# An earlier beginning, and the last four row blocks as rows, in a two-layer graph kernel

## The chip, the cores and the metric

The kernel runs on one core of one Trainium2 chip. The metric is the device time of one execution in microseconds. Four runs of the kernel before gave 2417.09 to 2418.88 us, with a median of 2418.69.

A core has five engines with a queue each: TensorE (matmuls, in profiles PE, its weight loads PEld), VectorE (DVE), ScalarE (ACT), GpSimd (POOL) and SyncE (SP), which here only issues transfers. Transfers are issued from the queues of SP, ScalarE and GpSimd.

## The reference, cut to what matters

There are 16 graphs of 1024 nodes with 128 features. Each goes through two layers, and each layer ends in a residual and a norm.

```python
# layer 0
h = x @ Ww.T + Wb
e = (h @ A) @ h.T;  e = e + e.T
att = softmax(where(adj > 0, e, 0), axis=1) * adj
hp = relu(att @ h)
i, f, o = (sigmoid(hp @ w_u + x @ w_x) for each of three gates)
x1 = layernorm(x + o * tanh(i * hp + f * x))          # eps 1e-5
# layer 1, four heads
h = x1 @ conv_w[hd] + conv_b[hd]
s = tanh(adj * (h @ attn_w[hd] @ h.T))
m = relu(mean over heads of relu(s @ h))
out = layernorm(x1 + relu(m + x1))                    # eps 1e-5
```

## The kernel before

A graph's 1024 nodes are eight blocks of 128. The kernel writes out the order of all instructions by hand; each engine works through its own in that order. Graph b's layer 1 is a loop over 32 steps (four heads of eight blocks, `layer1_step`), and between its steps stand pieces of layer 0 of the following graphs, named by letters in lists such as `"E1 S4 A0 T3"`: `L` load a block of adj, `E` find its edges (adj > 0), `Q` project to q, `H`/`h` multiply and add for h, `S` a row block of scores, `T` turn the part above the diagonal to below it, `A` mask with the edges, take the maximum and the exponential, `B` multiply with adj, divide and start the product with h. Graph 0 has no earlier graph to hide behind. Its layer 0 stands by itself at the start, and its order is in the two `run(first, ...)` lines.

**The beginning.** From A and Ww the kernel makes a_sym = A + A.T, s_ww = a_sym Ww and q_w = Ww.T s_ww, so that q = x q_w + c is one product. `keep_at_work(n)` gives TensorE n matmuls on zeros, whose result nobody reads. `finish_weights` adds the last column of wb_row and the gates' columns gate_x. A and Ww and Wb are loaded from ScalarE's queue, the three gate rows rows_x from GpSimd's, and xT, the eight blocks of adj, x and everything later from SP's. Graph 0's edges are found by VectorE, apart from blocks 5 and 6, which GpSimd finds. The turned copies of score block 0 wait in PSUM and are placed by VectorE (`place_first_score`, L397); those of the other blocks are copied by ScalarE (L376).

`small(...)` hands out four PSUM banks in turn, so a fifth request waits until the first has been read.

**The end.** Layer 1 sums the heads' results turned, features on partitions, in `sum_t`. For the last head of the last graph, tanh's results stay in `kept`. The first 512 nodes are multiplied within the steps. The other 512 follow in three parts, quarter (256 nodes), eighth and rest (128 each), by `last_back`: the head's h is stationary and `kept` moves, so the result has features on partitions; VectorE adds it to the sum (L667), and `last_end` turns it back on TensorE (L698), makes the residual on VectorE (L699, L702), and runs the norm. The norm takes statistics on VectorE (L221, L223, L225), the power -1/2 on GpSimd (L226), and applies both: on ScalarE for half and quarter (L232, L235), on VectorE for eighth and rest (L237). Its numbers are in the pools `mv` and `rs`, two buffers each, used in turn by all norms.

Of the kernel before, what the change touches and what calls it, by code (L numbers as in the profile page):

```python
# [11 lines left out]
F32 = mybir.dt.float32  # L12
# [3 lines left out]
ALU = mybir.AluOpType  # L16
# [8 lines left out]
def two_layer_adjacency_kernel(  # L25
# [48 lines left out]
    a_in = sb.tile([P, P], F32, tag="hz", name="a_in", bufs=4)  # L74
    nc.scalar.dma_start(a_in, A)
    ww_in = sb.tile([P, P], F32, tag="hz", name="ww_in", bufs=4)
    nc.scalar.dma_start(ww_in, Ww)
    wb_col = consts.tile([P, 1], F32, name="wb_col")

    wb_in = sb.tile([1, P], F32, tag="x1T", name="wb_in")  # L80
    nc.scalar.dma_start(wb_in, Wb.rearrange("(o d) -> o d", o=1))
    rows_x = sb.tile([3, P], F32, tag="s1", name="rows_x", bufs=4)
    for g, w in enumerate((wi_x, wf_x, wo_x)):
        nc.gpsimd.dma_start(rows_x[g : g + 1], w.rearrange("(o d) -> o d", o=1))
    rows_u = sb.tile([3, P], F32, tag="turn", name="rows_u", bufs=2)


# [53 lines left out]
        for _ in range(n):  # L141
            nc.tensor.matmul(idle[:, :P], warm[:, :P], warm[:, :P], start=True, stop=True)  # L142

    keep_at_work(7)
    pa, pb = small("p_a"), small("p_s")
    nc.tensor.transpose(pa[:, :P], a_in, ident)
    nc.vector.tensor_add(a_sym, pa[:, :P], a_in)
    keep_at_work(2)
    nc.tensor.matmul(pb[:, :P], a_sym, ww_in, start=True, stop=True)
    nc.vector.tensor_copy(s_ww, pb[:, :P])  # L150
    pc, pw = small("p_b"), small("p_ww")
    nc.tensor.transpose(pw[:, :P], ww_in, ident)
    nc.tensor.matmul(pc[:, P : P + 1], wb_in, ones[:, 0:1], start=True, stop=True)
    nc.tensor.matmul(pc[:, :P], ones, wb_in, start=True, stop=True)
    nc.vector.tensor_copy(wb_col, pc[:, P : P + 1])
    nc.scalar.copy(wwT, pw[:, :P])
    nc.scalar.copy(wb_row[:, :D], pc[:, :P])
    nc.gpsimd.tensor_copy(b_wide, wb_col.to_broadcast([P, P]))
    pq, pc = small("p_q"), small("p_c")
    nc.tensor.matmul(pq[:, :P], s_ww, ww_in, start=True, stop=True)  # L160
    nc.vector.tensor_copy(q_w, pq[:, :P])
    nc.tensor.matmul(pc[:, 0:1], s_ww, wb_col, start=True, stop=True)
    nc.tensor.matmul(pc[:, 1:2], a_sym, wb_col, start=True, stop=True)
    nc.vector.tensor_copy(c_col, pc[:, 0:1])
    nc.vector.tensor_copy(sb_col, pc[:, 1:2])
    keep_at_work(1)

    def finish_weights():
        pt = small("p_bsb")
        nc.tensor.matmul(pt[:, :1], b_wide, sb_col, start=True, stop=True)  # L170
        nc.tensor.matmul(pt[:, 1:4], rows_x, ident[:3, :3], start=True, stop=True)
        nc.vector.tensor_copy(wb_row[:, G - 1 : G], pt[:, :1])
        nc.vector.tensor_copy(gate_x, pt[:, 1:4])

    def turn_rows_u():
        pt = small("p_rows_u")
# [32 lines left out]
        if len(pending) > DELAY:  # L209
            pending.popleft()()  # L210

    def layernorm(t, dst, name, on_scalar=False):

        n = t.shape[1]
        st = sb.tile([P, n, nc.vector.BN_STATS_DIM], F32, tag="st", name=f"st_{name}")
        mv = sb.tile([P, n, 2], F32, tag="mv", name=f"mv_{name}")
        for k in range(n):  # L220
            nc.vector.bn_stats(st[:, k, :], t[:, k, :])  # L221
        for k in range(n):
            nc.vector.bn_aggr(mv[:, k, :], st[:, k, :])  # L223
        rs = sb.tile([P, n], F32, tag="rs", name=f"rs_{name}")
        nc.vector.tensor_scalar_add(rs, mv[:, :, 1], EPS)  # L225
        nc.gpsimd.tensor_tensor(rs, rs, mhalf[:, :n], ALU.pow)  # L226
        if on_scalar:
            nc.gpsimd.tensor_scalar_mul(mv[:, :, 0], mv[:, :, 0], -1.0)
        yield
        for k in range(n):  # L230
            if on_scalar:
                nc.scalar.activation(  # L232
                    dst[:, k, :], t[:, k, :], AF.Identity, bias=mv[:, k, 0:1]
                )
                nc.scalar.mul(dst[:, k, :], dst[:, k, :], rs[:, k : k + 1])  # L235
                continue
            nc.vector.tensor_scalar(  # L237
                dst[:, k, :], t[:, k, :], mv[:, k, 0:1], rs[:, k : k + 1],
                ALU.subtract, ALU.mult,
            )  # L240
# [54 lines left out]
    def layer0(b):  # L295
# [91 lines left out]
        def turn_first_score(half):  # L387

            ls = range(max(half * BH, 1), (half + 1) * BH)
            t["turned", half] = ps = small(f"turn0_0_{half}")  # L390
            for i, l in enumerate(ls):
                nc.tensor.transpose(ps[:, ts(i, P)], t["R"][:, l, 0, :], ident)  # L392

        def place_first_score():
            for half in range(NH):
                ls = range(max(half * BH, 1), (half + 1) * BH)
                nc.vector.tensor_copy(  # L397
                    t["R"][:, 0, ls[0] : ls[-1] + 1, :],
                    t["turned", half][:, : len(ls) * P].rearrange("p (l d) -> p l d", d=P),
                )  # L400

        def find_edges(j):

            if b == 0:
                m = sb.tile([P, N], BF16, tag="h1", name=f"edge_{b}_{j}", bufs=NB + 1)
            else:
                m = sb.tile([P, N], U8, tag="edge", name=f"edge_{b}_{j}")
            engine = nc.vector if b == 0 and j not in (5, 6) else nc.gpsimd
            engine.tensor_scalar(m, adj_t[b, j], 0.0, None, ALU.is_gt)  # L409
            t["edge", j] = m.rearrange("p (k d) -> p k d", d=P)  # L410

# [13 lines left out]
        def weigh(j):  # L425

            s = t["R"][:, :, j, :]
            adj = adj_t[b, j].rearrange("p (k d) -> p k d", d=P)
            rz = sb.tile([P, 1], F32, tag="rz", name=f"rz_{b}_{j}", bufs=4)
            t["hz", j] = sb.tile([P, D], F32, tag="hz", name=f"hz_{b}_{j}", bufs=4)  # L430
            if (b, j) != (0, NB - 1):
                nc.vector.tensor_mul(s, s, adj)  # L432
            nc.vector.reciprocal(rz, t["z", j])
            if b == 0 and j >= NB - 2:
                nc.vector.tensor_scalar_mul(t["hz", j], t["h"][:, j, :D], rz)
            else:
                nc.scalar.mul(t["hz", j], t["h"][:, j, :D], rz)
            if (b, j) == (0, NB - 1):
                for ks in (ts(0, BH), ts(1, BH)):
                    nc.vector.tensor_mul(s[:, ks], s[:, ks], adj[:, ks])  # L440
            if j:
                back(j - 1)

# [116 lines left out]
            "W": load_xT, "X": load_x, "R": relu,  # L560
        }
        if b == 0:
            pieces.update(P=lambda: rows_hp(GROUPS), G=gates, t0=place_first_score)
            for q in range(NH):
                pieces[f"T0.{q}"] = partial(turn_first_score, q)
                pieces[f"S1.{q}"] = partial(score, 1, [q])
# [99 lines left out]
        else:  # L666
            nc.vector.scalar_tensor_tensor(o, a, 0.0, o, op0=ALU.max, op1=ALU.add)  # L667

    def last_back(acc, ms, at):

        for m in ms:
            nc.tensor.matmul(  # L672
                acc, h1_t[B - 1, m][:, ts(H - 1, D)], kept[0][:, m, at : at + acc.shape[1]],
                start=(m == 0), stop=(m == NB - 1),
            )
        if ms[-1] == NB - 1:
            add_head(B - 1, H - 1, acc, at)

    def layer1_end(b):
        x1 = x1_t[b][:, :, 1 : D + 1]  # L680
# [10 lines left out]
    def last_end(b, k0, k1):  # L691
# [8 lines left out]
            y, pt.rearrange("p (k d) -> p k d", d=D), 1.0 / H, x1, op0=ALU.mult, op1=ALU.add  # L700
        )
        nc.vector.scalar_tensor_tensor(y, y, 0.0, x1, op0=ALU.max, op1=ALU.add)  # L702
        yield from layernorm(y, y, f"1_{b}_{k0}", on_scalar=n > 1)
        rows = out[b, k0 * P : k1 * P, :]
        nc.sync.dma_start(rows.rearrange("(k p) d -> p k d", p=P), y)

# [6 lines left out]
    load_late_weights()  # L713
    run(second, "L0 L1 L2 L3 L4 L5 L6 L7")
    run(first, "E0 Q0")
    keep_at_work(1)
    finish_weights()
    run(first, "H0 h0 E1 E2 E5 E6 S0 T0.0 S1.0 T0.1 S1.1 A0 t0 E3 T1 S2 A1 E4 H1 h1 B0 Q1 T2 S3 A2")
    run(first, "B1 H2 h2 T3 S4 A3 E7 B2")
    turn_rows_u()  # L720
    run(first, "T4 S5 A4 B3 T5 S6 A5 B4 T6 S7 A6")
    run(second, "Q0")
    run(first, "B5 A7")
    run(second, "H0")
# [10 lines left out]
    run(second, "H2 S1")  # L735
    run(first, "I1")
    next(join, None)
    run(second, "S2")
    run(first, "O0 V0 O1")
    run(second, "h2 S3 Q1")  # L740
    run(first, "N0")
    turn_first_x1(x1_t[0], 0)
    run(first, "V1 N1")
    head_uT(0, 0, [0])
    rows(0, range(0, 2))
# [29 lines left out]
    for b in range(B):  # L775
        plan = BETWEEN if b else {**BETWEEN, **FIRST}
        after = layer0(b + 2) if b + 2 < B else {}
        for step in range(H * NB):
# [8 lines left out]
            if step == TURN and b + 1 < B:  # L787
                turn_x1(b + 1)
            run(after, AHEAD.get(step, ""))
            if hd == H - 1 and b + 1 < B:  # L790
                if m == NB - 1:
                    head_uT(b + 1, 0)
# [5 lines left out]
        end = layer1_end(b)  # L798
    while pending:
        pending.popleft()()  # L800
    cuts = ((0, 4), (4, 2), (6, 1), (7, 1))
    half, quarter, eighth, rest = (last_end(B - 1, k, k + n) for k, n in cuts)
    acc_q = ps_acc.tile([P, N], F32, tag="acc0", name="acc_q")[:, : 2 * P]
    last_back(acc_q, range(0, 2), 4 * P)
    next(half)
    last_back(acc_q, range(2, NB), 4 * P)
    acc_e = ps_acc.tile([P, N], F32, tag="acc1", name="acc_e")[:, :P]
    last_back(acc_e, range(0, 4), 6 * P)
    next(quarter)
    next(half, None)  # L810
    last_back(acc_e, range(4, NB), 6 * P)
    acc_r = small("acc_r")[:, :P]
    last_back(acc_r, range(0, 4), 7 * P)
    next(eighth)
    next(quarter, None)
    last_back(acc_r, range(4, NB), 7 * P)
    next(rest)
    next(eighth, None)
    next(rest, None)
# [38 lines left out]
```

## Time and profile before

| | us |
|---|---|
| median of 4 runs | 2418.69 |
| the profiled execution | 2418.64 |
| its span in the profile | 2416.6 |
| TensorE / VectorE / ScalarE / GpSimd busy | 2404.1 / 1555.3 / 1074.0 / 611.8 |
| first layer-1 score on TensorE (L643) starts | 70.56 |
| last operation of a compute engine (L237) starts | 2413.72 |

The span runs from the first instruction to the last event; 2.04 us of the execution's time lie outside it. Rows of a timeline give start, duration, engine, line, operation, output<-input, shape and count; in brackets stands the idle time of the engine before it and what ended it. Several instructions of one kind in a row are one row. A matmul in float32 is two passes, and each pass is one instruction of the profile. Line numbers are those of the kernel before.

### The profile page before, as it was taken

How to read it: one execution, taken by the hardware profiler on the slowest of the kernel's cores; microseconds unless marked ns; L12 is line 12 of the kernel's file. 1: busy time of each engine (PE TensorE's matmuls, PEld its weight loads, DVE VectorE, ACT ScalarE, POOL GpSimd, SP SyncE). 2: the span in 40 equal slices, each digit the busy share in tenths (PEclk: the TensorE clock that was granted, in tenths of full speed). 3: DMA queues.
4: the chain of work that ended last, by engine and by line, in shares of the span. 5: the costliest groups of instructions: out<-in, count | busy, mean ns of one | idle time of the engine just before them, and what ended most of it. 6: DMA issues, size and time to landing. Idle time of an engine off the chain costs nothing.

```text
span 2416.6 us, 20226 instructions
## 1 busy us (share of the span) xinstructions
PE 2404.1 (99%) x5980; PEld 1098.0 (45%) x5980; DVE 1555.3 (64%) x3280; ACT 1074.0 (44%) x1505; POOL 611.8 (25%) x379
## 2 busy tenths in 40 slices
PE   9999999999999999999999999999999999999998
PEld 5444444444444444444444444444444444444444
DVE  6756676666666666676566665666666576666554
ACT  5544344453444534445344454444444344443333
POOL 1314141241312413123131331312214132141000
PEclk9999999999999999999999999999999999999999
DMA  4334151341514414143242432425234251341010
GB/s 180 79 72 122 35 138 44 86 123 38 137 36 97 112 48 126 46 104 95 60 115 52 114 79 70 105 61 122 61 72 112 52 130 54 79 116 31 18 27 9
DMA packets 473308, 196.71 MB, mean 81 GB/s; under 512 B 414442, under 2 KB 439278, under 8 KB 473199
## 3 DMA queue, kind: packets, MB, share of 16 engines
q1 hardware_dynamic: 454525, 128.70, 22.7%
q0 software_dynamic: 18384, 66.59, 9.0%
q8 instruction: 47, 0.77, 0.1%
q14 instruction: 62, 0.51, 0.1%
q10 hardware_dynamic: 290, 0.13, 0.0%
HBM read 135.86 MB, written 59.51 MB: 81 GB/s over the span
## 4 chain that ended last, share of the span: by engine, by line
PE 99%; DVE 1%; ACT 0%; issue 0%; POOLq 0%; DVEq 0%; ACTq 0%
PE sc L643 36%; PE acc L649 36%; PE acc L448 9%; PE sc L357 5%; PE pR L614 5%; PE pT_u L246 5%; PE pR_h L338 1%; PE pT_q L246 1%; DVE R L416 0%; PE idle L142 0%; PE acc_q L672 0%; DVE R L432 0%; PE pt L467 0%; DVE edge L409 0%; PE pt L606 0%
## 5 line engine op out<-in xcount | busy, mean ns | idle before, releaser
L644 DVE TENSOR_TENSOR s<-sc,adj 128x512 f32<-128x512 f32 x1008 | 684.9, 687 | 711.7 <-PE sc L643 690.5
L645 ACT ACTIVATE s<-s 128x1024 f32<-128x1024 f32 x504 | 533.1, 1058 | 1032.0 <-DVE s L644 1031.8
L643 PE MATMUL sc<-uT,x1T 128*128 128x512 f32 x2048 | 962.4, 592 | 0.0
L649 PE MATMUL acc<-s,h 128*128 128x512 f32 x2016 | 947.3, 592 | 0.0
L649 PEld LDWEIGHTS acc<-s,h 128*128 128x128 f32 x2016 | 380.5, 190 | 484.7 <-issue 477.0
L643 PEld LDWEIGHTS sc<-uT,x1T 128*128 128x128 f32 x2048 | 387.0, 190 | 469.8 <-issue 404.0
L409 POOL TENSOR_SCALAR edge<-adj 128x1024 uint8<-128x1024 f32 (+1 forms) x122 | 339.2, 2780 | 322.6 <-DVE top_None L416 314.1
L226 POOL TENSOR_TENSOR rs<-rs,mhalf 128x8 f32<-128x8 f32 (+3 forms) x36 | 55.1, 1531 | 948.7 <-DVE rs L225 948.7
L448 PE MATMUL acc<-R,hz 128*128 128x512 f32 x512 | 241.4, 594 | 0.1
L423 ACT ACTIVATE R<-R,nmax 128x1024 f32<-128x1024 f32 x128 | 146.9, 1148 | 74.9 <-DVE nmax L421 71.9
L416 DVE CUSTOM_DVE_ANT_0 R<-R,edge 128x1024 f32<-128x1024 f32 (+1 forms) x128 | 154.6, 1208 | 0.7 <-PE turn L392 0.5
L432 DVE TENSOR_TENSOR R<-R,adj 128x1024 f32<-128x1024 f32 x127 | 154.1, 1214 | 0.0
L448 PEld LDWEIGHTS acc<-R,hz 128*128 128x128 f32 x512 | 97.4, 191 | 123.4 <-issue 117.6
L357 PE MATMUL sc<-xT,qT 128*128 128x512 f32 (+3 forms) x384 | 146.3, 489 | 2.9 <-ACT qT L250 1.7
L360 ACT ACTIVATE R<-sc,h 128x512 f32<-128x512 f32 (+1 forms) x192 | 110.7, 579 | 53.7 <-PE sc L357 48.5
L480 POOL TENSOR_TENSOR x1T<-hp,wu_b 128x1024 f32<-128x1024 f32 x45 | 107.8, 2396 | 102.3 <-DVE hws L486 63.1
L246 PE MATMUL pT_u<-x1T,ms 128*128 128x512 f32 x256 | 120.6, 592 | 0.7 <-ACT x1T L607 0.7
L614 PE MATMUL pR<-cw,x1T 128*128 128x512 f32 x256 | 117.6, 598 | 0.0
L357 PEld LDWEIGHTS sc<-xT,qT 128*128 128x128 f32 x384 | 69.7, 191 | 72.4 <-issue 59.6
L312 POOL DMA_DIRECT2D adj<-in_adjT_dram x112 | 65.5, 585 | 92.6 <-DVE s L644 92.6
L667 DVE SCALAR_TENSOR_TENSOR sum<-acc,sum 128x512 f32<-128x512 f32 x95 | 61.2, 686 | 42.2 <-PE acc L649 42.2
L617 ACT COPY h<-pR 128x512 f32<-128x512 f32 x128 | 72.3, 592 | 28.3 <-PE pR L614 26.6
(149 smaller groups left out, 1137.6 us busy)
## 6 DMA issues: line engine op xcount, KB each, us to landing
adj<-in_adjT_dram POOLq DMA_DIRECT2D x112, 512.0 KB, 4.0
adj<-in_adjT_dram SPq DMA_DIRECT2D x16, 512.0 KB, 7.4
x<-in_x_dram SPq DMA_DIRECT2D x16, 512.0 KB, 5.4
xT<-in_xT_dram SPq DMA_DIRECT2D x15, 512.0 KB, 10.7
dram_hp<-turn_hp SPq DMA_DIRECT2D x15, 512.0 KB, 2.6
hp<-dram_hp SPq DMA_DIRECT2D x60, 128.0 KB, 3.1
dram_x<-turn_x SPq DMA_DIRECT2D x15, 512.0 KB, 2.8
x1T<-dram_x SPq DMA_DIRECT2D x60, 128.0 KB, 5.9
```

What stands on the lines that cost most here:

```text
L246: nc.tensor.matmul(ps, w, src[:, ts(q, 512)], start=True, stop=True)
L357: nc.tensor.matmul(ps[:, : at - lo], t["qT"][:, ts(j, P)], t["xT"][:, lo:at], start=True, stop=True)
L409: engine.tensor_scalar(m, adj_t[b, j], 0.0, None, ALU.is_gt)
L416: nc.vector.tensor_tensor_reduce(s[:, ks], s[:, ks], t["edge", j][:, ks], 1.0, nmax, ALU.mult, ALU.max, top)
L423: nc.scalar.activation(s, s, AF.Exp, bias=nmax, accum_out=t["z", j])
L432: nc.vector.tensor_mul(s, s, adj)
L448: nc.tensor.matmul(t["acc"][:, ts(q, 512)], t["hz", j], t["R"][:, ts(q, BH), j, :], start=(j == 0), stop=(j == NB - 1),)
L614: nc.tensor.matmul(ps, x1T_t[b][:, ts(k, P)], cw.rearrange("p h d -> p (h d)"), start=True, stop=True)
L643: nc.tensor.matmul(ps, x1T[:, ts(m, P)], uT[:, ts(q, 512)], start=True, stop=True)
L644: nc.vector.tensor_mul(s[:, ts(q, 512)], ps, adj[:, ts(q, 512)])
L645: nc.scalar.activation(s, s, AF.Tanh)
L649: nc.tensor.matmul(acc[:, ts(q, 512)], h1[:, ts(hd, D)], s[:, ts(q, 512)], start=(m == 0), stop=(m == NB - 1),)
```

## The change

It touches the two ends of the program; the loop between them keeps its order, but for the reciprocal in `weigh`, which now stands ahead of the product with adj.

In the beginning, Ww and Wb are loaded from SP's queue ahead of xT, and rows_x from ScalarE's. The fillers on TensorE become seven instead of eleven, and the small products are put in another order. gate_x has a PSUM bank of its own and is made ahead of the first edge. All edges of graph 0 are found by VectorE. The turned block 0 is copied by ScalarE. E1 stands ahead of h, Q1 ahead of E4 and H1, E5 and E6 stand later, and the second graph's h2 and Q1 change places.

At the end, the last head's second 512 nodes are multiplied with `kept` stationary and the head's h moving, so that the result has nodes on partitions. `ready_last` runs in step 28 and turns the sum of the three earlier heads, with 4·x1 added (`base`), and keeps 4·x1 (`x`). `last_rows` then makes 4 times the residual, and its norm has an eps 16 times as large. Quarter's norm is applied by VectorE. Half's norm keeps its numbers in a tile of its own (`own`).

```diff
-    nc.scalar.dma_start(ww_in, Ww)
+    nc.sync.dma_start(ww_in, Ww)
-    nc.scalar.dma_start(wb_in, Wb.rearrange("(o d) -> o d", o=1))
+    nc.sync.dma_start(wb_in, Wb.rearrange("(o d) -> o d", o=1))
...
-        nc.gpsimd.dma_start(rows_x[g : g + 1], w.rearrange("(o d) -> o d", o=1))
+        nc.scalar.dma_start(rows_x[g : g + 1], w.rearrange("(o d) -> o d", o=1))
...
-    keep_at_work(7)
-    pa, pb = small("p_a"), small("p_s")
+    keep_at_work(6)
+    pa, pw, pb, ps = small("p_a"), small("p_ww"), small("p_b"), small("p_s")
     nc.tensor.transpose(pa[:, :P], a_in, ident)
     nc.vector.tensor_add(a_sym, pa[:, :P], a_in)
-    keep_at_work(2)
-    nc.tensor.matmul(pb[:, :P], a_sym, ww_in, start=True, stop=True)
-    nc.vector.tensor_copy(s_ww, pb[:, :P])
-    pc, pw = small("p_b"), small("p_ww")
     nc.tensor.transpose(pw[:, :P], ww_in, ident)
...
     nc.gpsimd.tensor_copy(b_wide, wb_col.to_broadcast([P, P]))
-    pq, pc = small("p_q"), small("p_c")
+    nc.tensor.matmul(ps[:, :P], a_sym, ww_in, start=True, stop=True)
+    nc.vector.tensor_copy(s_ww, ps[:, :P])
+    pc, pq, px = small("p_c"), small("p_q"), small("p_x")
+    nc.tensor.matmul(pc[:, 1:2], a_sym, wb_col, start=True, stop=True)
+    keep_at_work(1)
     nc.tensor.matmul(pq[:, :P], s_ww, ww_in, start=True, stop=True)
     nc.vector.tensor_copy(q_w, pq[:, :P])
     nc.tensor.matmul(pc[:, 0:1], s_ww, wb_col, start=True, stop=True)
-    nc.tensor.matmul(pc[:, 1:2], a_sym, wb_col, start=True, stop=True)
...
-    keep_at_work(1)
+    nc.tensor.matmul(px[:, :3], rows_x, ident[:3, :3], start=True, stop=True)
+    nc.vector.tensor_copy(gate_x, px[:, :3])
...
-    def layernorm(t, dst, name, on_scalar=False):
+    def layernorm(t, dst, name, on_scalar=False, eps=EPS, own=False):
...
+        if own:
+            numbers = sb.tile([P, 3 * n], F32, tag="gate", name=f"numbers_{name}")
+            mv = numbers[:, : 2 * n].rearrange("p (k t) -> p k t", t=2)
+            rs = numbers[:, 2 * n :]
...
-            t["turned", half] = ps = small(f"turn0_0_{half}")
+            ps = small(f"turn0_0_{half}")
...
+            nc.scalar.copy(
+                t["R"][:, 0, ls[0] : ls[-1] + 1, :],
+                ps[:, : len(ls) * P].rearrange("p (l d) -> p l d", d=P),
+            )
...
-            engine = nc.vector if b == 0 and j not in (5, 6) else nc.gpsimd
+            engine = nc.gpsimd if b else nc.vector
...
-            if (b, j) != (0, NB - 1):
-                nc.vector.tensor_mul(s, s, adj)
             nc.vector.reciprocal(rz, t["z", j])
...
+            for ks in (ts(0, BH), ts(1, BH)) if (b, j) == (0, NB - 1) else [slice(NB)]:
+                nc.vector.tensor_mul(s[:, ks], s[:, ks], adj[:, ks])
...
+    def ready_last(b):
+        x1 = x1_t[b][:, BH:, 1 : D + 1]
+        both = sb.tile([P, 2, BH, D], F32, tag="hp", name="base", bufs=1)
+        last["base"], last["x"] = both[:, 0], both[:, 1]
+        pt = small("pt_base")
+        for i in range(BH):
+            nc.tensor.transpose(pt[:, ts(i, P)], sum_t[b][:, ts(BH + i, P)], ident)
+        nc.vector.scalar_tensor_tensor(
+            last["base"], x1, float(H), pt.rearrange("p (k d) -> p k d", d=D),
+            op0=ALU.mult, op1=ALU.add,
+        )
+        nc.scalar.mul(last["x"], x1, float(H))
...
+    def last_back(acc, i, k, ms=range(NB)):
         for m in ms:
             nc.tensor.matmul(
-                acc, h1_t[B - 1, m][:, ts(H - 1, D)], kept[0][:, m, at : at + acc.shape[1]],
+                acc[:, ts(i, D)], kept[0][:, m, ts(k, P)], h1_t[B - 1, m][:, ts(H - 1, D)],
                 start=(m == 0), stop=(m == NB - 1),
             )
-        if ms[-1] == NB - 1:
-            add_head(B - 1, H - 1, acc, at)
...
+    def last_rows(b, acc, k0, k1):
+        n, at = k1 - k0, slice(k0 - BH, k1 - BH)
+        y = sb.tile([P, n, D], F32, tag="s1", name=f"y_{b}_{k0}", bufs=4)
+        nc.vector.scalar_tensor_tensor(
+            y, acc.rearrange("p (k d) -> p k d", d=D), 0.0, last["base"][:, at],
+            op0=ALU.max, op1=ALU.add,
+        )
+        nc.vector.scalar_tensor_tensor(y, y, 0.0, last["x"][:, at], op0=ALU.max, op1=ALU.add)
+        yield from layernorm(y, y, f"1_{b}_{k0}", eps=EPS * H * H)
+        rows = out[b, k0 * P : k1 * P, :]
+        nc.sync.dma_start(rows.rearrange("(k p) d -> p k d", p=P), y)
...
-    run(first, "E0 Q0")
-    keep_at_work(1)
+    run(first, "E0 Q0")
     finish_weights()
-    run(first, "H0 h0 E1 E2 E5 E6 S0 T0.0 S1.0 T0.1 S1.1 A0 t0 E3 T1 S2 A1 E4 H1 h1 B0 Q1 T2 S3 A2")
-    run(first, "B1 H2 h2 T3 S4 A3 E7 B2")
+    run(first, "E1 H0 h0 E2 S0 T0.0 S1.0 T0.1 S1.1 A0 E3 T1 S2 A1 Q1 E4 H1 h1 B0 T2 S3 A2 E5 B1")
+    run(first, "H2 h2 T3 S4 A3 E6 B2")
     turn_rows_u()
-    run(first, "T4 S5 A4 B3 T5 S6 A5 B4 T6 S7 A6")
+    run(first, "T4 S5 A4 E7 B3 T5 S6 A5 B4 T6 S7 A6")
...
-    run(second, "S2")
+    run(second, "h2 S2")
     run(first, "O0 V0 O1")
-    run(second, "h2 S3 Q1")
+    run(second, "S3")
     run(first, "N0")
     turn_first_x1(x1_t[0], 0)
+    run(second, "Q1")
...
+            if b + 1 == B and step == (H - 1) * NB + 4:
+                ready_last(b)
...
+    last_back(acc_q, 0, BH, range(0, 4))
     next(half)
+    last_back(acc_q, 0, BH, range(4, NB))
+    last_back(acc_q, 1, BH + 1)
+    quarter = last_rows(B - 1, acc_q, BH, BH + 2)
     next(quarter)
     next(half, None)
+    last_back(acc_e, 0, BH + 2)
+    eighth = last_rows(B - 1, acc_e, BH + 2, BH + 3)
     next(eighth)
     next(quarter, None)
+    last_back(acc_r, 0, BH + 3)
+    rest = last_rows(B - 1, acc_r, BH + 3, BH + 4)
     next(rest)
     next(eighth, None)
     next(rest, None)
```

## The prediction

> **What bounds the kernel now.** I read the page first: busy shares, then the chain that ended last.
>
> ```profile
> PE 2404.1 (99%) x5980; PEld 1098.0 (45%) x5980; DVE 1555.3 (64%) x3280; ACT 1074.0 (44%) x1505; POOL 611.8 (25%) x379
> ...
> PE 99%; DVE 1%; ACT 0%; issue 0%; POOLq 0%; DVEq 0%; ACTq 0%
> ```
>
> TensorE is the path nearly throughout. Where it isn't, I looked with the busy time by stage (columns: length, then busy us of PE, PEld, DVE, ACT, POOL, granted clock, DMA share, GB/s):
>
> ```profile
> 105.00:400.00 295.00, 295.00 (x724) 133.64 (x723) 187.39 (x381) 132.26 (x184) 77.44 (x46) 1.00 0.33 84
> 400.00:2300.00 1900.00, 1900.00 (x4637) 859.01 (x4636) 1234.75 (x2601) 839.56 (x1158) 493.70 (x296) 1.00 0.32 81
> ...
> 22.00:23.00 1.00, 0.00 (x0) 0.00 (x0) 1.00 (x2) 0.94 (x3) 0.00 (x0) 1.00 0.07 20
> 23.00:24.00 1.00, 0.91 (x1) 0.45 (x2) 0.96 (x4) 0.95 (x4) 0.00 (x0) 0.59 0.07 19
> 24.00:25.00 1.00, 1.00 (x3) 0.43 (x2) 0.55 (x2) 0.00 (x0) 0.00 (x0) 0.50 0.07 20
> 25.00:26.00 1.00, 1.00 (x3) 0.48 (x2) 0.00 (x0) 0.85 (x2) 0.00 (x0) 0.50 0.07 20
> ```
>
> TensorE never stops from 70 to 2400 us (the 70 to 105 row reads 35.00 of 35.00 too). So a microsecond won before 70 or after 2400 goes straight to the end, and nothing in between can be won by VectorE or ScalarE. In the beginning TensorE starves around 22 us and the granted clock then halves until about 26.5 us. The third view is the timeline of the two stages that change:
>
> ```profile
> 13.34 6.46 POOL L409 TENSOR_SCALAR edge<-adj 128x1024 bf16<-128x1024 f32 x2 [6.03 <-DMA adj<-in_adjT_dram]
> ...
> 15.43 1.14 DVE L397 COPY R<-turn 128x384 f32<-128x384 f32 x2
> ...
> 17.09 2.06 DVE L416 CUSTOM_DVE_ANT_0 R<-R,edge 128x1024 f32<-128x1024 f32 x1
> ...
> 19.27 1.08 DVE L409 TENSOR_SCALAR edge<-adj 128x1024 bf16<-128x1024 f32 x1
> ...
> 28.12 0.43 DVE L342 TENSOR_TENSOR h<-pR_h,wb_row 128x264 f32<-128x264 f32 x1 [3.57 <-PE pR_h L338]
> ...
> 32.03 1.23 DVE L416 CUSTOM_DVE_ANT_0 R<-R,edge 128x1024 f32<-128x1024 f32 x1
> ```
>
> While GpSimd finds edges 5 and 6 (13.34 to 19.80), the same VectorE operation takes 2.06 instead of 1.23 us and an edge 1.08 instead of 0.68. Then VectorE idles 3.57 us behind slow matmuls.
>
> **The beginning, part by part.**
>
> *The way to q.* The old order had two fillers between a_sym and p_s; now p_ww, the two p_b and p_s fill that place, and six instead of seven fillers stand ahead. A filler is two passes of 0.215 to 0.24 us there (four passes took 1.06 at 4.40). One filler less: p_a at 3.76 instead of 4.19. Then p_ww 0.21, p_b 0.27 and 0.40, p_s 0.43, drain 0.2, copy s_ww 0.29, p_q 0.45, so q_w starts near 6.4 instead of 7.22. The first q then waits only for p_c and p_x: 6.75 instead of 7.78. Gain 0.8 to 1.0.
>
> *DMA queues.* Ww and Wb leave ScalarE's queue for the head of SP's, ahead of xT, all eight adj, x and everything later; each issue took about 0.45 there, so xT and adj start up to 0.9 late. rows_x leaves GpSimd for ScalarE's queue (three issues of 0.45; the table load follows at about 2.7 instead of 2.2 and still ends at 4.0, before the first ScalarE copy near 4.4). When does adj land? GpSimd waited for adj 5 until 13.3; summing the GB/s per microsecond, the bytes up to adj 5 had passed at 12.3, so landing is about 1 us behind the bytes. The same sum puts adj 0 at 6.4 and adj 1 at 8.1. Shifted by 0.6 (0 to 0.9): 7.0 and 8.7. Edge 0 then runs at 7.0, edge 1 (now queued ahead of h on VectorE) at 8.7 to 9.4, h at 9.3 to 9.9, instead of 11.51 when it ended. Scores of block 0 are evicted from 9.95 (was 11.74) and the first mask starts at 11.4 (was 13.19): **gain 1.7**. Bounds: 2.2 if adj isn't late, 0.9 at a shift of 1.4; behind edge 1 stand h and all ScalarE evictions, so this wait is passed on in full. The later loads on SP shift by up to 0.9 too, unseen: the next ones needed, rows_u and cw_last, were issued by 13.3 and 28.2 and are wanted near 25 and 35.
>
> *Mask 0 to mask 7 on VectorE* took 13.19 to 39.95, 26.8 us. Out go: the excess beside GpSimd, 0.38 (mask 0's second half, 1.07 against 0.69), 0.83 (mask 1) and 0.40 (edge 4), 1.6 together; the two copies L397, 1.0, now ScalarE copies of about 0.46 and 0.58 in ScalarE's slack; the idle 3.57. In come edges 5 and 6, 0.6 of spacing each, 1.2. That would leave 21.8. Laying the instructions end to end by these rows leaves waits: mask 1 still waits about 1.0 for score, transposes and copies of block 1 (and ScalarE now carries the copies), smaller ones make another 1.1. So 23.9: **gain 2.9**, mask 7 at 35.3. The idle 3.57 goes because qT's second half now comes off ScalarE ahead of hz 0 (near 18.1, was 22.37), so scores of block 3 follow at 18.9, not 20.9 to 23.1. After mask 7 TensorE has less backlog (blocks 5 and 6 are multiplied as they come, not in one run of 5.42): **gain 0.6**. The same laying-out on the old order, with the measured slow rows and half clock, ends the transposes of hp at 49.97; the trace has 49.85. So 49.85 becomes about 44.7.
>
> [...]The fillers are there for the clock. [...]Passes here ran at 0.215 to 0.24 until about 5.9 and at 0.11 from 6.7. Four of eleven fillers go. [...]I take 0, since real matmuls fill the place without a gap. [...]19.6 to 23.0 wasn't idle but busy 0.74 of 3.40, in gaps of 1.0 and 1.7. In the new order the emptiest 3.4 us hold 2.3 of work, so I expect no drop; one would give 1.5 back.
>
> [...]
>
> *47 to 61 us.* h2 of the second batch moves ahead of O0, into a VectorE wait of 0.52 for tanh, so the first norm starts at 58.7 (bounded by GpSimd's pow), not 58.99; Q1's 0.86 moves into TensorE's wait for the x1T copy (60.5 to 61.16). **Gain 0.3**. The reciprocal ahead of the product, in all batches, costs nothing: z is a step old by then.
>
> **The end.** Four base transposes, 0.45, join a stage where TensorE is the bound: **loss 0.45**. The base operation (0.69) and ScalarE's 4·x (0.6) lie in gaps of 1.0 and 1.5 per step. The first half keeps its chain, 0.46 later. Rows cost TensorE no more: sixteen passes of 256 took 3.45, thirty-two of 128 cost 32 x 0.1125 = 3.6. VectorE now sets the end:
>
> ```profile
> 2410.76 0.28 DVE L667 SCALAR_TENSOR_TENSOR sum<-acc_r,sum 128x128 f32<-128x128 f32 x1
> ...
> 2411.09 0.14 PEld L698 LDWEIGHTS pt<-ident,sum 128*128 128x128 f32 x1 [1.18 <-DVE sum L667]
> ...
> 2411.46 0.29 DVE L699 SCALAR_TENSOR_TENSOR y<-pt,x 128x128 f32<-128x128 f32 x1 [0.42 <-PE pt L698]
> ...
> 2413.72 0.34 DVE L237 TENSOR_SCALAR y<-y,mv,rs 128x128 f32<-128x128 f32 x1 [0.48 <-POOL rs L226]
> ```
>
> Three sums and three transposes go (the last pair alone was 2410.76 to 2411.46). Half's numbers end at 2406.35; quarter from 2406.26 (neighbours overlap by 0.09), spaced as before (0.46, 0.45, 0.41, 0.33, 0.08), to 2407.99; eighth 1.45, to 2409.44; the quarter's two norms, now on VectorE, 0.56; rest from 2410.0 (its matmuls end at 2409.7) to 2411.52; pow 0.57; last norm at 2412.26, was 2413.72: 1.46, the 0.45 included. The four stores follow each other more closely; I take 0.15 off. **Gain 1.3** (0.8 to 1.5). Own places for mean and factor free VectorE from ScalarE's reads; before that cost about 0.1.
>
> **Sum.** 1.7 + 2.9 + 0.6 + 0.3 + 1.3 = 6.8, less 0.2 for the half-clock passes ahead of q: 6.6. The profiled execution took 2418.64 (span 2416.6); its median is 2418.69, 0.05 above. So 2412.1.
>
> **Rivals.**
> - *Arrival binds.* adj 1 lands past 10, or p_x, which stands ahead of the first q on TensorE, waits for rows_x (landing took 4.5 to 5.6 from GpSimd; from ScalarE only Wb bounds it, at most 3.8 after its issue). For: the queues move 230 to 426 GB/s in every microsecond from 3 to 15. Against: no edge on VectorE waited for adj before. Gain 3 to 5: about 2414.5.
> - *The clock drops again*, early or near 20: gain 4 to 5.2, about 2414. Against: the 2.3 of 3.4 above.
> - *Slower: the reciprocal as a new wait.* In fifteen batches it stands ahead of the product, behind ScalarE's accumulator read (0.19). If it is late, TensorE's eviction queues behind it on VectorE. 120 x 0.19 = 23 at worst, 2435; it decides from 0.06 us for each. Against: z is a step old, and L644 idles 711.7 us in all.
> - *The middle swallows it* (a transfer fixed in time): only the end remains, 2417.4. Against: the second adj set is issued by 37 and used from 57.
>
> **How the numbers follow.** About 0.2% (4.8 us) is what a measurement of this kernel tells from no change: below 2413.85 is faster. Forecast 0.70 (2410.6 to 2413.4, nearly all faster); arrival 0.14 and clock 0.08 (a third of each faster); swallowed 0.04; slower 0.04. Faster 0.77, same 0.19, slower 0.04. Range 2410.4 to 2414.8.
>
> **What would show it.** Right: no GpSimd edge before 50, mask 1 at 1.23 to 1.3, granted clock 1.00 from 20 to 30, hp's transposes ending near 44.7, the first layer-1 score near 65, the last norm 1.46 nearer to the last layer-1 score than before. Wrong: an edge waiting for adj, p_x waiting, a clock below 1.00, or TensorE gaps behind 70.

## Result and profile after

| | before | after |
|---|---|---|
| median, us (runs) | 2418.15 (61) | 2414.42 (41) |
| profiled execution / its span, us | 2418.64 / 2416.6 | 2415.03 / 2412.9 |

The ratio is 0.9984, with a 95% interval of 0.9979 to 0.9988: 3 to 5 us, or 0.12 to 0.21%. The direction was right and the time lies in the range, but it is 2.3 above the forecast of 2412.1, and the gain is 0.16% of the time before, a little less than the 0.2% that was set as the bound for "faster".

The 41 executions are not spread evenly. Eleven took 2411.96 to 2412.84, thirty 2414.27 to 2415.25, and none lies between (the expectation of e8 below counts one wrongly, 12 and 29). The profiled one belongs to the second group. This is the key to the case.

The page of the kernel after, busy shares and the chain that ended last:

```profile
PE 2404.1 (100%) x5988; PEld 1099.1 (46%) x5988; DVE 1553.3 (64%) x3280; ACT 1064.0 (44%) x1504; POOL 603.4 (25%) x373
...
PE 99%; DVE 1%; ACT 0%; issue 0%; POOL 0%; POOLq 0%; DVEq 0%; ACTq 0%
```

The kernel after by stage (length, busy us of PE, PEld, DVE, ACT, POOL, granted clock, DMA share, GB/s):

```profile
22.00:23.00 1.00, 1.00 (x4) 0.50 (x4) 1.00 (x2) 1.00 (x4) 0.00 (x0) 1.00 0.07 19
...
105.00:2300.00 2195.00, 2195.00 (x5359) 992.61 (x5358) 1421.12 (x2978) 961.36 (x1339) 571.18 (x342) 1.00 0.33 82
```

TensorE no longer starves at 22 us, the clock stays at 1.00 there (in every row from 20 to 29), and from 105 on TensorE is full as before. That is as predicted. The beginning is not. TensorE's rows in the timeline of the kernel after:

```profile
3.98 0.42 PE L148 MATMUL p_ww<-ident,ww_in 128*128 128x128 f32 x1
4.33 0.58 PE L150 MATMUL p_b<-ones,wb_in 1*128 1x1 f32 x2
4.78 0.77 PE L151 MATMUL p_b<-wb_in,ones 1*128 1x128 f32 x2
...
8.21 2.08 PE L327 MATMUL pT_q_first<-xT,q_w 128*128 128x512 f32 x2
...
10.36 1.67 PE L341 MATMUL pR_h<-wwT_g,xT 128*128 128x132 f32 x6
11.82 2.75 PE L360 MATMUL sc<-xT,qT 128*128 128x512 f32 x4
```

The same work in the trace of before, and below it mask 0, the masking of score block 0 with its edges on VectorE (mask 1 is that of block 1, and so on):

```profile
7.78 1.02 PE L324 MATMUL pT_q_first<-xT,q_w 128*128 128x512 f32 x2
...
10.68 1.88 PE L357 MATMUL sc<-xT,qT 128*128 128x512 f32 x4
...
13.19 0.69 DVE L416 CUSTOM_DVE_ANT_0 R<-R,edge 128x512 f32<-128x512 f32 x1 [0.47 <-PE turn L392]
```

Two passes of the first q take 2.08 us; in the trace of before they took 1.02. Six passes for h take 1.67 (before 0.91). The four of the first scores take 2.75 where 1.88 is normal; an excess of 0.87 is two passes at twice their length, so TensorE changes to full rate near 13.5 us. In the trace of before it did so near 5.9. The granted clock does not show it. Every such row of the kernel after up to 16 us has a granted clock (third number from the end) of 1.00, as this one has:

```profile
8.00:10.00 2.00, 2.00 (x4) 1.03 (x4) 0.79 (x3) 0.00 (x0) 0.00 (x0) 1.00 0.99 395
```

Only the lengths of the passes show the rate. VectorE's rows show what the half rate costs:

```profile
8.39 0.68 DVE L408 TENSOR_SCALAR edge<-adj 128x1024 bf16<-128x1024 f32 x1
...
12.12 0.57 DVE L345 TENSOR_TENSOR h<-pR_h,wb_row 128x396 f32<-128x396 f32 x1 [0.83 <-PE pR_h L341]
...
15.20 0.69 DVE L415 CUSTOM_DVE_ANT_0 R<-R,edge 128x512 f32<-128x512 f32 x1 [1.90 <-PE turn L395]
...
18.57 1.23 DVE L415 CUSTOM_DVE_ANT_0 R<-R,edge 128x1024 f32<-128x1024 f32 x1 [0.76 <-PE turn L378]
```

Mask 0 starts at 15.20; before it was 13.19, and 11.4 was forecast. Every idle time here ends on TensorE, none on a transfer. Mask 1 takes 1.23, as predicted.

Three later rows of the kernel after mark where the beginning goes on: mask 7, the turning of hp, and the first layer-1 score.

```profile
38.04 1.22 DVE L415 CUSTOM_DVE_ANT_0 R<-R,edge 128x1024 f32<-128x1024 f32 x1
...
45.84 2.05 PE L464 MATMUL pt<-ident_g,hpT 128*128 128x131 f32 x16
...
68.28 1.88 PE L640 MATMUL sc<-uT,x1T 128*128 128x512 f32 x4
```

The end of the kernel after, from the last matmuls within the steps to the last norm:

```profile
2398.55 1.12 PE L646 MATMUL acc<-kept,h 128*128 128x512 f32 x2 [0.16 <-ACT kept L642]
...
2409.59 0.35 DVE L240 TENSOR_SCALAR y<-y,mv,rs 128x128 f32<-128x128 f32 x1 [0.48 <-POOL rs L229]
```

That is 11.04 us. Before, the same stretch took 13.31, from this row of the chain that ended last to the last norm at 2413.72:

```profile
2400.41 1.13 PE acc L649 x2
```

The span ends 3.31 after the last norm starts, before 2.88: the stores take 0.43 more.

So the profile has a loss of 2.0 up to mask 0 and a gain of 5.7 from there on (spans less the start of mask 0: 2403.4 and 2397.7). Two questions follow: what keeps TensorE at half rate, and where do the 5.7 come from?

### The profile page after: what moved, and what is told of

It is laid out like the page before. It is cut to its first block, busy times and chain, and to the rows that moved or that the text cites. A ratio compares the mean times of both kernels' runs of the same rounds, so it can differ in the third digit from the quotient of the medians.

```text
span 2412.9 us, 20181 instructions
## 1 busy us (share of the span) xinstructions
PE 2404.1 (100%) x5988; PEld 1099.1 (46%) x5988; DVE 1553.3 (64%) x3280; ACT 1064.0 (44%) x1504; POOL 603.4 (25%) x373
## 3 DMA queue, kind: packets, MB, share of 16 engines
q1 hardware_dynamic: 454671, 128.77, 22.8%
## 4 chain that ended last, share of the span: by engine, by line
PE 99%; DVE 1%; ACT 0%; issue 0%; POOL 0%; POOLq 0%; DVEq 0%; ACTq 0%
PE sc L640 36%; PE acc L646 36%; PE acc L445 9%; PE sc L360 5%; PE pR L611 5%; PE pT_u L249 5%; PE pR_h L341 1%; PE pT_q L249 1%; PE idle L142 0%; DVE st L225 0%; DVE R L415 0%; DVE u L533 0%; PE pt L464 0%; PE pT_q_first L327 0%; PE pt L603 0%
## 5 line engine op out<-in xcount | busy, mean ns | idle before, releaser
L408 POOL TENSOR_SCALAR edge<-adj 128x1024 uint8<-128x1024 f32 x120 | 332.7, 2772 | 316.5 <-DVE top_None L415 314.0
L315 POOL DMA_DIRECT2D adj<-in_adjT_dram x112 | 65.6, 586 | 92.5 <-DVE s L641 92.5
```

## Experiments

"Late" means in the following an execution of 2414.2 us or more by a kernel with the new order and the new end.

**1. Are the missing fillers the cause?** The four fillers are put back in the changed kernel (e1):

```diff
-    keep_at_work(6)
+    keep_at_work(7)
...
     nc.vector.tensor_add(a_sym, pa[:, :P], a_in)
+    keep_at_work(2)
     nc.tensor.transpose(pw[:, :P], ww_in, ident)
...
     run(first, "E0 Q0")
+    keep_at_work(1)
     finish_weights()
```

> The changed kernel with the four warm-up passes back (seven ahead of p_a, two behind it, one behind the first q). The changed kernel measured 2414.4; in its trace TensorE ran at half rate until about 13 us. Theory 1 (the fillers kept the array busy enough[...]): half rate ends near 6 as before, although q starts about 0.9 later than in the new order without them; mask 0 near 12.0 to 12.5 instead of 15.20, mask 1 near 15.5; time about 2412 to 2412.5. Theory 2[...]: half rate ends as late as in the changed kernel in as many executions, and the extra passes cost their own length: 2414.5 to 2415.5.

Measured: 2412.45 (ratio 0.9975, 0.9965 to 0.9985); of nine executions one is late. Rows of the timeline of this kernel, TensorE, VectorE and ScalarE:

```profile
4.33 0.61 PE L142 MATMUL idle<-warm 128*128 128x128 f32 x4
...
7.41 1.10 PE L328 MATMUL pT_q_first<-xT,q_w 128*128 128x512 f32 x2
...
8.32 0.69 DVE L409 TENSOR_SCALAR edge<-adj 128x1024 bf16<-128x1024 f32 x1 [0.71 <-DMA adj<-in_adjT_dram]
9.80 0.69 DVE L409 TENSOR_SCALAR edge<-adj 128x1024 bf16<-128x1024 f32 x1 [0.72 <-DMA adj<-in_adjT_dram]
10.40 0.56 DVE L346 TENSOR_TENSOR h<-pR_h,wb_row 128x396 f32<-128x396 f32 x1
...
11.06 1.27 ACT L364 ACTIVATE R<-sc,h 128x512 f32<-128x512 f32 x2 [1.68 <-DVE h L346]
...
12.51 0.69 DVE L416 CUSTOM_DVE_ANT_0 R<-R,edge 128x512 f32<-128x512 f32 x1 [0.74 <-PE turn L396]
```

With four more matmuls on zeros the median is 2.0 lower. (The two ratio intervals overlap, but one late execution of nine against thirty of forty-one is hardly chance, and experiment 6 adds to both counts.) Full rate begins near 4.4, q comes 0.8 *earlier* than without them, and mask 0 is 2.7 earlier. Now a wait that half rate had hidden appears: both edges wait 0.7 for adj, h stands behind the second, and ScalarE's first copy of the scores waits for h until 11.06. That copy started 1.06 after the first score's beginning in the trace of before (10.68, 11.74); by this, an estimate, it could start at 10.5 here, so the wait costs about 0.5.

**2. The other way round: the old way to q in the changed kernel** (e4: queues, weight products and fillers as before, all else as after). Against the changed kernel, in short:

```diff
-    nc.sync.dma_start(ww_in, Ww)
+    nc.scalar.dma_start(ww_in, Ww)
...
-    keep_at_work(6)
+    keep_at_work(7)
...
     nc.vector.tensor_add(a_sym, pa[:, :P], a_in)
+    keep_at_work(2)
+    nc.tensor.matmul(pb[:, :P], a_sym, ww_in, start=True, stop=True)
+    nc.vector.tensor_copy(s_ww, pb[:, :P])
...
     nc.tensor.transpose(pw[:, :P], ww_in, ident)
```

> The changed kernel with the old way to q (queues, weight passes, their order and all eleven fillers as before; the edges on VectorE, ScalarE's copies, the new order of the steps and the end stay). Theory 1: half rate ends near 6, q at 7.8 as before, edge 1 not later than h, so h near 11.0 to 11.5 and mask 0 near 13.0 instead of 15.20; hp's transposes end near 46 instead of 47.9; time 2412.5 to 2413.3, less than the changed kernel's 2414.4 although q is later. Theory 2 and the theory that adj's arrival binds: no gain over the changed kernel, 2414.4 to 2415.2.

Measured: 2412.41 (0.9974, 0.9964 to 0.9984), no late execution of eight. Mask 0 starts at 13.00. A slower written order with its fillers beats the quicker one without them.

**3. The fillers taken from the kernel before** (e2: 6, 0, 1, 0 instead of 7, 2, 1, 1):

```diff
-    keep_at_work(7)
+    keep_at_work(6)
...
-    keep_at_work(2)
...
     run(first, "E0 Q0")
-    keep_at_work(1)
```

> The kernel before with the changed kernel's filler counts (six ahead of p_a instead of seven, none behind it, none behind the first q) and nothing else changed. Before measured 2418.15. Theory 1: it loses the warm-up as the changed kernel did: half rate until 9 or 13 us, mask 0 later than 13.19 by about 1 to 2.5; time 2419 to 2420.5. Theory 2: the passes left out were pure delay: 2417.5 to 2418.2, mask 0 near 12.9.

Measured: median 2419.68, but the ratio, 1.0000 (0.9992 to 1.0008), is unclear. The profile is not: the first q takes 1.91 at 8.78, full rate begins near 16.3, and mask 0 starts at 17.22, not 13.19.

```profile
17.22 0.99 DVE L415 CUSTOM_DVE_ANT_0 R<-R,edge 128x512 f32<-128x512 f32 x1 [1.46 <-PE turn L391]
```

Eight of its thirteen executions took over 2419.5, of the kernel before beside it twelve of forty. Why the time rose so little with mask 0 4 us later is taken up below the table that sets all profiles side by side.

**4. Which of them, and is it chance?** Only the two behind p_a (e6), and the changed kernel once more, unchanged (e8). The edit of e6:

```diff
     nc.vector.tensor_add(a_sym, pa[:, :P], a_in)
+    keep_at_work(2)
     nc.tensor.transpose(pw[:, :P], ww_in, ident)
```

> The changed kernel with only the two warm-up matmuls between p_a and p_ww put back (six ahead of p_a, none behind the first q). [...]Theory 1 (the weak stretch from 3.8 to 5.5[...]): these two repair it, 2412.0 to 2412.5, mask 0 near 12.2. If the filler ahead of p_a or the one behind the first q is what counts: 2414.5 to 2415.3.

> The changed kernel once more, unchanged, beside the others. Of its 41 executions 12 took 2411.96 to 2412.84 and 29 took 2414.27 to 2415.25, with none between. Theory 1[...] the same two groups appear again. If the two groups come from something else (the placement of transfers), the group of 2412 differs from the filler kernel in more than the start of full rate.

Measured: e6 2415.11 (0.9985, 0.9978 to 0.9991), eleven of twenty-one late; e8 2414.30 (0.9982, 0.9975 to 0.9988), twelve of twenty-one late, so the two groups are there again: 2411.58 to 2412.72 and 2414.28 to 2415.15. Two fillers alone were not enough. The early executions of the changed kernel take what e1 takes, with fewer passes ahead of q. No early execution of it was profiled; that TensorE was at full rate in them is inferred. But in every late profile of the new order (after, e6, e7, e8) the first q takes 2.08, and in every early one (e1, e4, e5, e10, e11, e12) 1.02 to 1.12. The profile of e8 is again one of the late ones, but it changes rate near 12.0, not 13.5, and takes 2414.28, not 2415.03: the instant differs from execution to execution.

**5. Which passes count?** The four restored fillers as transposes (e5), and all eleven as matmuls over a single row (e9); both stand on e1:

```diff
+    def turn_at_work(n):
+        for _ in range(2 * n):
+            nc.tensor.transpose(idle[:, :P], warm[:, :P], ident)
...
-    keep_at_work(7)
+    keep_at_work(6)
+    turn_at_work(1)
...
-    keep_at_work(2)
+    turn_at_work(2)
...
-    keep_at_work(1)
+    turn_at_work(1)
     finish_weights()
```

```diff
-            nc.tensor.matmul(idle[:, :P], warm[:, :P], warm[:, :P], start=True, stop=True)
+            nc.tensor.matmul(idle[:, :P], ones, ones, start=True, stop=True)
```

> As the kernel with the four warm-up passes restored (2412.45, half rate over by 4.5 to 5, mask 0 at 12.51), but the four restored ones are transposes of the same 128x128 tile, two for each so that they take as long. Theory 1a (it is the kind of work that counts[...]): half rate lasts to 9 or 13 us in most executions, time 2414.5 to 2415.2. Theory 1b (any passes without a gap will do; the changed kernel was only short of passes): 2412.3 to 2412.7.

> The kernel with the four warm-up passes restored, but all eleven warm-up matmuls take one row of ones instead of 128 rows (same number, same 128x128 result, same length of a pass). Theory 1a' (one-row passes do not keep the array busy[...]): [...]half rate until 9 to 13 us in every execution, nothing under 2414. Theory 1b (what counts is an unbroken row of passes of any kind): as with the 128-row ones, eight in ten executions near 2412.5 and the rest near 2416.

Measured: e5 2412.56 (0.9981, 0.9974 to 0.9989), two of fourteen late. e9 2419.33 (1.0006, 0.9998 to 1.0014), all thirteen at 2418.58 or more. Rows of e9's timeline:

```profile
1.17 3.35 PE L142 MATMUL idle<-ones 1*128 1x128 f32 x14 [1.17 <-DVE ones L68]
...
10.68 2.08 PE L328 MATMUL pT_q_first<-xT,q_w 128*128 128x512 f32 x2
...
15.32 3.62 PE L361 MATMUL sc<-xT,qT 128*128 128x512 f32 x4
18.73 0.58 PE L396 MATMUL turn<-ident,R 128*128 128x128 f32 x3
```

Fourteen one-row passes in the place of fourteen full ones, just as long (3.35 in both) and without a gap between them, and the half rate lasts until 18.8. So what counted here was how many rows a pass uses (none of thirteen executions early with one row, eight of nine with 128 in e1), not that TensorE is issuing. Transposes, of 128 rows too and two in the place of each filler, did about as well as matmuls (2412.56 for 2412.45). The stretch from 4.33 to 5.5 in the changed kernel, the p_b rows, is of one-row passes, and this is where the old order had two fillers and p_s. No run moved the p_b rows alone, with the number of fillers unchanged, so how much of the loss is theirs stays open. The prediction's "real matmuls fill the place without a gap" was true and beside the point.

**6. Full passes only, up to p_q** (e12: p_ww, p_b and p_c behind p_q, fillers 7, 2, 2, 1). The new order of that place:

```python
keep_at_work(7)
nc.tensor.transpose(pa[:, :P], a_in, ident)
...
keep_at_work(2)
nc.tensor.matmul(ps[:, :P], a_sym, ww_in, start=True, stop=True)
...
keep_at_work(2)
nc.tensor.matmul(pq[:, :P], s_ww, ww_in, start=True, stop=True)
...
nc.tensor.transpose(pw[:, :P], ww_in, ident)
...
keep_at_work(1)
nc.tensor.matmul(pc[:, 1:2], a_sym, wb_col, start=True, stop=True)
```

> The changed kernel with p_ww, the p_b rows and the p_c columns put behind p_q, and seven, two, two and one warm-up matmuls ahead of p_a, p_s, p_q and p_c, so that up to p_q TensorE has only full 128-row passes and hardly a gap. The first q comes about 0.9 later than in the kernel with four passes restored. Theory 1[...]: no late execution or one of twenty, all near 2413.0 to 2413.5. If the late executions have another cause, two in ten stay near 2416.5.

Measured: 2412.67 (0.9978, 0.9969 to 0.9986), twelve executions of 2412.42 to 2413.38, none late. Together: late were 42 of 62 with the changed kernel (its own runs and e8), 8 of 43 with the four fillers back (e1, e7, e10), 0 of 12 here. Where both kinds ran beside each other, it was 12 of 21 (e8) against 8 of 35 (e5, e7). That none of twelve was late here is no proof that this order is safer than e1's: at a share of 8 in 43, twelve in a row without one have a chance of about 0.08.

The traces give the instant at which full rate begins. In e10 it is near 4.1, 3.1 after TensorE's first pass at 1.04; in e1 and e3 it is near 4.4, in before near 5.9, and in e12 between 6.5 and 6.9 (its fillers at 5.68 still take 0.21 a pass; p_ww at 6.91 takes 0.27, where it takes 0.42 at half rate). The late profiles change rate near 12.0 (e8), 13.3 (e7) and 13.5 (after, e6), e2 near 16.3 and e9 near 18.8; no profile does so between 7 and 12. What sets the instant no run shows, so why one execution of a kernel is early and the next late stays open; the counts show only that the share of late ones changes with what TensorE does ahead of q (42 of 62 and 8 of 43).

**7. What GpSimd's edges cost.** e1 with edges 5 and 6 back on GpSimd, at their old place (e10), and the kernel before with the new end alone (e3: `own`, `ready_last`, `last_rows` and the last lines of the diff). The edit of e10 on e1:

```diff
-            engine = nc.gpsimd if b else nc.vector
+            engine = nc.vector if b == 0 and j not in (5, 6) else nc.gpsimd
...
-    run(first, "E1 H0 h0 E2 S0 T0.0 S1.0 T0.1 S1.1 A0 E3 T1 S2 A1 Q1 E4 H1 h1 B0 T2 S3 A2 E5 B1")
-    run(first, "H2 h2 T3 S4 A3 E6 B2")
+    run(first, "E1 H0 h0 E2 E5 E6 S0 T0.0 S1.0 T0.1 S1.1 A0 E3 T1 S2 A1 Q1 E4 H1 h1 B0 T2 S3 A2 B1")
+    run(first, "H2 h2 T3 S4 A3 B2")
```

> The kernel with the four warm-up passes restored, and edges 5 and 6 back on GpSimd, asked for where the kernel before asks for them. Prediction's terms: the same VectorE operations beside GpSimd's edges lose 1.6 in all (mask 1 at 2.06 instead of 1.23) and VectorE is spared 1.2, so 0.4 slower than the kernel with its edges on VectorE (2412.45), 2412.9. If the loss beside GpSimd is small in most executions (the kernel before with the new end alone showed mask 1 at 1.22 beside the same edges), it is 0 to 1.2 faster: 2411.3 to 2412.4, and the move to VectorE was no gain in itself.

> The kernel before with the changed end alone (rows out of TensorE, own numbers), beginning and middle as before. From the two traces the stretch from the start of the last layer-1 matmul group to the last norm is 13.31 before and 11.04 after, 2.27 shorter, against 0.45 for the four base transposes and 0.43 that the stores take longer: about 1.4, so 2416.7. If the end brings 0.5 or less, the beginning brought nearly all of the 3.7; if it brings over 2.5, the beginning brought only about 1.

e10 measured 2411.86 (0.9975, 0.9966 to 0.9983); twelve of thirteen took 2411.28 to 2412.20, one was late. It is the lowest median of all the kernels, 0.6 below e1, though the intervals do not separate the two. Rows of its timeline:

```profile
15.77 1.23 DVE L416 CUSTOM_DVE_ANT_0 R<-R,edge 128x1024 f32<-128x1024 f32 x1 [0.76 <-PE turn L379]
17.11 1.11 DVE L409 TENSOR_SCALAR edge<-adj 128x1024 bf16<-128x1024 f32 x1
...
14.88 5.96 POOL L409 TENSOR_SCALAR edge<-adj 128x1024 bf16<-128x1024 f32 x2 [8.73 <-DMA adj<-in_adjT_dram]
```

Beside the same GpSimd operations mask 1 takes 1.23 here, and only edge 4 is longer, 1.11 for 0.68. The 2.06 of the trace of before need not come. No run shows a gain from moving the edges to VectorE.

e3 measured 2417.10 against 2418.81 (0.9993, 0.9986 to 0.9999). Its profiled execution, 2413.75, is the quickest of its twenty-one, which go up to 2419.29. It has the old order with GpSimd's edges, and no slow mask in it either:

```profile
16.17 1.22 DVE L421 CUSTOM_DVE_ANT_0 R<-R,edge 128x1024 f32<-128x1024 f32 x1
```

Only edge 4 beside GpSimd is longer, 1.33. It also starves TensorE at 20 us. By stage:

```profile
19.00:20.00 1.00, 0.66 (x4) 0.30 (x2) 1.00 (x2) 0.05 (x1) 1.00 (x1) 1.00 0.14 35
20.00:21.00 1.00, 0.00 (x0) 0.00 (x0) 1.00 (x3) 0.45 (x2) 0.01 (x1) 1.00 0.07 22
21.00:22.00 1.00, 0.42 (x1) 0.30 (x2) 0.96 (x4) 1.00 (x3) 0.00 (x0) 1.00 0.07 20
...
24.00:25.00 1.00, 1.00 (x8) 0.76 (x8) 0.09 (x1) 0.85 (x3) 0.00 (x0) 1.00 0.07 20
```

TensorE is busy 1.08 of 3.00 us, yet the clock stays at 1.00. In the trace of before it was busy 0.48 of 3.00 (20 to 23 us) when the clock dropped. So the second drop, too, came in the profiled execution of before and not in this one, which starved less; no run shows whether that decided it.

**8. Is adj's arrival passed on?** e1 with h ahead of edge 1 (e7), and the same with the old way to q (e11):

```diff
-    run(first, "E1 H0 h0 E2 S0 T0.0 S1.0 T0.1 S1.1 A0 E3 T1 S2 A1 Q1 E4 H1 h1 B0 T2 S3 A2 E5 B1")
+    run(first, "H0 h0 E1 E2 S0 T0.0 S1.0 T0.1 S1.1 A0 E3 T1 S2 A1 Q1 E4 H1 h1 B0 T2 S3 A2 E5 B1")
```

> The kernel with the four warm-up passes restored, and h ahead of edge 1 on VectorE (in the trace of that kernel edge 1 waited 0.72 for adj and h stood behind it until 10.40, though its matmuls had ended near 9.5). Theory (adj's arrival is passed on to h): h near 9.7, mask 0 near 11.8 instead of 12.51, time 2411.7 to 2411.9 against 2412.45. Rival (something else ends last there: mask 1 waits for the transposes of block 1, or edge 1 comes late for it): 2412.3 to 2412.6.

> The changed kernel with the old way to q (2412.41 in eight executions, none of them late) and h ahead of edge 1. If the old order of the weight passes, with a product of full rows behind the fillers, is safer than the new one with the same fillers (seven late executions of thirty there): 0 to 2 late ones of twenty, median 2412.0 to 2412.5. If the order does not matter: three to six of twenty near 2416, the median still 2412.2 to 2412.6.

e7: 2412.57 (0.9982, 0.9975 to 0.9988), six of twenty-one late; the other fifteen took 2411.60 to 2412.72, e1's eight took 2411.95 to 2413.28. A gain of the 0.6 expected is not excluded and not shown. The profiled execution was a late one, where adj is no limit, so the trace does not decide either. e11: 2412.67 (0.9982, 0.9973 to 0.9991), one of eleven late; with e4, one of nineteen for the old order of the weight products against eight of forty-three for the new one with as many fillers. That is a hint, no more.

**All profiles side by side.** The first column is what the beginning takes, the last what everything behind it takes (span less first column):

| kernel | mask 0 starts | span | rest |
|---|---|---|---|
| before | 13.19 | 2416.6 | 2403.4 |
| e2, before with fewer fillers | 17.22 | 2417.5 | 2400.3 |
| e3, before with the new end | 12.58 | 2411.8 | 2399.2 |
| after | 15.20 | 2412.9 | 2397.7 |
| e8, after again | 14.44 | 2412.2 | 2397.8 |
| e1, four fillers back | 12.51 | 2410.3 | 2397.8 |
| e9, one-row fillers | 19.46 | 2417.4 | 2397.9 |
| e4, old way to q | 13.00 | 2410.6 | 2397.6 |
| e5, four fillers as transposes | 12.48 | 2410.2 | 2397.7 |
| e6, two fillers back | 15.58 | 2413.3 | 2397.7 |
| e7, e1 with h first | 15.98 | 2413.7 | 2397.7 |
| e11, e4 with h first | 13.27 | 2410.8 | 2397.5 |
| e12, full passes first | 13.36 | 2411.1 | 2397.7 |
| e10, edges on GpSimd | 12.40 | 2409.9 | 2397.5 |

With the new order and end the rest is 2397.5 to 2397.9, whether mask 0 starts at 12.4 or at 19.5: what the beginning wins or loses goes to the end in full. In the old order the rest differs by 3.1 between two profiles with the same instructions from there on (before, e2). What differs in their rows are the slow operations beside GpSimd and the second clock drop. Behind the start of mask 0 the one has 1.6 of slow operations and a drop that the prediction put at 1.5; the other has a first half of mask 0 of 0.99 for 0.69 and no drop (clock 1.00 from 15 to 28). That makes 2.8 of the 3.1. In e2 mask 0 comes so late that mask 1 runs behind GpSimd's edges; in e3 it runs beside them and is not slow either. By these two profiles this is also why e2 lost so little; only one profile of each was taken.

The stretch behind mask 0 can be split by rows of the two traces:

| from, to | forecast gain | before | after | gain |
|---|---|---|---|---|
| mask 0 to mask 7 | 2.9 | 26.8 | 22.8 | 3.9 |
| mask 7 to the end of the hp transposes | 0.6 | 9.90 | 9.85 | 0.05 |
| from there to the first layer-1 score | 0.3 | 20.7 | 20.4 | 0.3 |
| first layer-1 score to the end of the span | 1.3 | 2346.0 | 2344.6 | 1.4 |

## Why the prediction was right and wrong

- **The way to q: failed, and it is the step that failed.** The prediction put the price of four fillers less at zero ("I take 0, since real matmuls fill the place without a gap") and took 0.2 off for all half-rate passes. Measured: mask 0 at 15.20 where the same order with the fillers has 12.51, so 2.7, in about two of three executions (42 of 62 were late). The forecast of 2412.1 is 0.3 to 0.5 from what the kernel takes when full rate comes early (the early executions have a median of 2412.6, in e8 2412.4; e1 2412.45). That it comes so near is in part luck: in e1 mask 0 gains 0.7 where 1.7 was forecast, and the stretch behind it 5.6 where 5.1 was. The forecast by itself reached from 2410.6 to 2413.4; that the median lies in the range at all is owed to the room left for the rivals near 2414.
- **Arrival of adj: mis-sized, hidden by the half rate.** Landing was put at 7.0 and 8.7; e1 has edges starting on adj's landing at 8.32 and 9.80. The kernel before with the new end started edge 0 at 7.56, on landing too, where the prediction had 6.4 for the old queues. By these two profiles the shift was near its upper bound (0.8 of 0.9), and the landing had been put 1.2 too early. With q at 7.41 (with the fillers) for 6.75, this is what the rows show behind mask 0 at 12.5 in e1 and not at 11.4; no run took the wait away and won the time.
- **Mask 0 to the end: near in sum, wrong in its parts.** The prediction had 2.9, 0.6, 0.3 and 1.3, 5.1 in all; the profiles have 3.9, 0.05, 0.3 and 1.4, 5.7. The smaller backlog behind mask 7, put at 0.6, brought 0.05: VectorE still waits there for TensorE's next h, 2.81 after and 2.63 before. And up to 3.1 of the 3.9 belongs to the profiled execution of before. From mask 0 to the first layer-1 score e2 takes 54.2, e3 54.8, after 53.1, so against these two the new order brings 1.1 and 1.7. The term for the operations beside GpSimd, 1.6 out and 1.2 in, was read from one trace, and e10 shows no gain in it.
- **The end: right.** 1.3 was forecast (0.8 to 1.5). From the first layer-1 score to the end of the span before and e2 take 2346.0, e3 2344.4, after 2344.6, e1 2344.7: a gain of 1.4 to 1.6, the base transposes and the stores included. e3 by its medians gives 1.7, by its ratio 0.2 to 3.4. Two parts were mis-sized and cancel: the last norm came 2.27 nearer to the last product of the steps, where 1.91 was forecast (1.46 and the base's 0.45), and the stores took 0.43 more, where 0.15 was.
- **No clock drop near 20, mask 1 at 1.23, TensorE full from 70: right.** That no edge waited for adj holds in the late profile alone; in e1 two do. The hp transposes end at 47.9 in the late profile and at 45.2 in e1; 44.7 was forecast; the first layer-1 score comes at 68.3 and 65.6, where 65 was.
- **The rivals.** "The clock drops again, early or near 20" named the right place, with about 2414 and a chance of 0.08; its "early" half is what happened, though as a full rate that came late (near 12.0 and 13.5 in the profiles of this kernel), not as a drop. "Arrival binds" is there once the clock is right, for about 0.5 by the estimate of experiment 1, which experiment 8 neither shows nor excludes. The reciprocal as a new wait cost nothing that shows: TensorE is busy 2195.00 of 2195.00 us in the loop.

## What to carry to other kernels

Matmuls on zeros whose result nobody reads can have a function: without four of the eleven, mask 0 came 2.7 us later here (15.20 for 12.51) in about two of three executions. When real instructions take their place, ask how many rows each pass uses (with eleven of one row the half rate lasted to 18.8 us, with 128 rows in e1's profile to 4.4), and not only whether the queue has gaps, and read the rate from the length of a known pass (here 1.02 or 2.08 for the first q). If a kernel's executions fall into groups, count the groups before the medians are compared; a profile shows one execution of one group. And a stall that only one trace shows, a slow operation beside GpSimd (here 2.06 for 1.23) or a dropped clock (0.50), belongs into the sum with the share of executions that have it.

## Not expected of the hardware

- One-row passes did not end the half rate: with all eleven fillers of one row it lasted to 18.8 us, and no execution of thirteen was early, 2419.33 for the 2412.45 with 128-row ones; 128-row transposes in the place of four of the eleven did no harm (2412.56).
- The granted clock in the profile read 1.00 throughout the first half-rate phase of the kernel after, while two 512-column passes took 2.08 instead of 1.02; in the later drop of the kernel before it read 0.50.
- The same mask beside the same GpSimd edges took 2.06 in one profile and 1.22 and 1.23 in two others (e3, e10). What decides it between executions is open.
